# Attention and a nonlocal block in FP32: quarters of q, v and k added by accumulating transfers, another order of steps in a pair, and other readers of the plain product

## The chip, the cores and the metric

The kernel runs on one core of a Trainium2 chip. Its engines work side by side, each on its own queue of instructions: TensorE (PE; its weight loads are shown as PEld), VectorE (DVE), ScalarE (ACT), GpSimd (POOL), and SyncE (SP), which here only issues transfers. Transfers run on 16 DMA engines. TensorE writes to PSUM; VectorE and ScalarE read it from there. The metric is the device time of one execution in microseconds, lower is better. Before the change the median of three runs is 2135.65 us (2135.11 to 2136.66).

## The reference

The input x has 8 images of 512 channels and 32 x 32 positions, all in FP32. Two layers follow each other:

```python
# layer 0: attention with 8 heads of d = 64 over n = 1024 positions
q, k, v = (conv1x1(x, W, b).reshape(B, h, d, n) for W, b in ((Wq, bq), (Wk, bk), (Wv, bv)))
attn = softmax(einsum('bhdn,bhdm->bhnm', q, k) * d ** -0.5, axis=-1)
x = x + conv1x1(einsum('bhnm,bhdm->bhdn', attn, v), Wp, bp)
# layer 1: nonlocal block, then normalization over the batch
g, theta, phi = (conv1x1(x, w, b) for each of the three)      # 256 channels
f = einsum('bcn,bdn->bcd', theta, phi) / n
z = conv1x1(einsum('bcd,bdn->bcn', f, g), W_w, W_b) + x
out = (z - mean(z)) * rsqrt(var(z) + eps) * gamma + beta      # over batch and positions
```

## The kernel before

The images are worked through one after the other. In the loop over `b` (L1008) each image goes through attention; then q, v and k of the *next* image are computed (L1053, L1058, L1069); then the projection of this image's attention output, theta and phi, and the nonlocal block. So there are seven seams, one between each two images, in which q, v and k of the next image are made, and they are the place of this change.

All matrix products by weights use Strassen's scheme in Winograd's form: a product of 2 x 2 blocks by seven block products. For q, v and k of the seams (`six`, L352) it is used twice, one inside the other. The operands' quarters are called 11, 12, 21, 22, and their sums t1 to t4. Of the seven outer products one, 11 by 11, is the *plain product* (`plain`, L373): it goes straight to PSUM in two halves. The other six go in three pairs (`SIX`, L349), the two outer products of a pair side by side; each of them is again seven inner products. A *step* is one of these seven for both members of the pair, and `ORDER` (L350) says in which order the steps come.

An outer product has three accumulators in PSUM, called chains here (the fourth entry of a row of `SEVEN`, L271). Inner products of one chain are added up in place, and after each one VectorE or ScalarE reads the chain as it stands and adds it to (or puts it in) the quarters that need it at that moment. So the next product of a chain can only be written when the last state of it has been read. PSUM is used in four slots of two banks of 512 numbers each. A pair takes all four: chain 0 of member m is in the first bank of slot m, chain 1 in the first bank of slot 2 + m, chain 2 in the second bank of slot 2 + m (L409). The plain product uses two slots just before, and they become slots 2 and 3 of the first pair. In q, a fill between the second and the third pair sums up the softmax denominators in one more slot (L653) and takes their reciprocals (L655); that slot becomes slot 3 of the third pair.

The outer products' results go to the quarters of the result (11, 12, 21, 22) or to two temporary quarters, T6 and T7, which come from a pool of three buffers (`w3`, tag "acc"). The same pool holds the running sums of the exponentials in attention. Once the pairs are done, whole quarters are added to each other (`add`, L370), by GpSimd's elementwise addition of 128 x 1024 numbers: before the third pair 12 += 22 and 12 += T6 (L398, L399); at the end T7 += T6 (only in q), 22 += T7 and 21 += T7 (L431 to L434). In v and k T6 enters T7 when VectorE writes T7 (`third`, L516 and L546).

The plain product's two halves are read twice each (`begin`), for T6 and for 11: three of these reads by ScalarE, the fourth (second half, 11) by VectorE (L388 to L390; L508 in q and k, L545 in v). `fills` puts other work between the steps, in the order of the engine's queue: in q the sums t4 of the next image's x (L252) and the inner sums of t3 and t4 (L264), all on VectorE; in "middle" the denominators and the loads of their reciprocals r, repeated over partitions (L698, SyncE's queue); in v the products of the attention output o with r (L684, GpSimd); in k the sums of o for the projection (L252 and L264, GpSimd).

Instructions that go through `pe`, `dve` or `sp` keep their order in the program on their engine; GpSimd's adds go through `dve` as well, and so have a fixed place in GpSimd's queue. Accumulating transfers are used already for another thing: `together` (L614) puts the four partition groups of a sum of exponentials on each other, one by SyncE and three by GpSimd with `accum_op` (L617).

Of the kernel before, what the change touches and what calls it, by code (L numbers as in the profile page):

```python
# [10 lines left out]
AF = mybir.ActivationFunctionType  # L11
ALU = mybir.AluOpType
# [18 lines left out]
def unshifted(ctx: ExitStack, tc: tile.TileContext, a: dict, out: bass.AP):  # L31
    nc = tc.nc
# [32 lines left out]
    dve = sp = pe  # L65
# [281 lines left out]
                between[n]()  # L347

    SIX = (((1, "21", "11"), (6, "22", "12")), ((3, "t1", "22"), (4, "t2", "T6")), ((5, "t3", "T7"), (2, "t4", "21")))  # L349
    ORDER = (0, 1, 2, 5, 4, 3, 6)  # L350

    def six(name, w, data, positions_out, at, begin, third, fills, by_scalar=False):  # L352

        fills = dict(fills)
        shape = [P, 4, 256] if positions_out else [P, 2, 512]
        temps = {}

        def to(q):
            if q[0] != "T":
                return at(q)  # L360
            if q not in temps:
                temps[q] = w3.tile(shape, F32, tag="acc", name=f"{q}_{name}")
            return temps[q]

        def piece(q, i, j):
            if positions_out:
                return to(q)[:, j * 2:j * 2 + 2, i * P:(i + 1) * P]
            return to(q)[:, i, j * 256:(j + 1) * 256]

        def add(q, of, engine=None):  # L370
            dve((engine or nc.gpsimd).tensor_tensor(to(q), to(q), to(of), ALU.add))

        def plain():  # L373
            d = data["11"]
            for half in range(2):
                ps = next_bank(f"{name}_0_{half}")[:, 0, :]
                if positions_out:
                    ps = ps.rearrange("p (i f) -> p i f", f=256)
                for i in range(2 if positions_out else 1):
                    for k in range(2):  # L380
                        if positions_out:
                            at = (half * 2 + i) * P
                            pe(nc.tensor.matmul(ps[:, i, :], d[:, k, at:at + P], w[:, 0, k, :],  # L383
                                                start=(k == 0 and i == 0), stop=(k == 1), skip_group_check=True))
                        else:
                            pe(nc.tensor.matmul(ps, w[:, 0, k, half * P:(half + 1) * P], d[:, k, :],  # L386
                                                start=(k == 0), stop=(k == 1), skip_group_check=True))
                for q in ("T6", "11"):  # L388
                    at_ = to(q)[:, half * 2:half * 2 + 2, :] if positions_out else to(q)[:, half, :]
                    begin(at_, ps, half, half and q == "11")  # L390
            load_w("first")

        plain()
        for one in fills.pop("plain", ()):
            one()
        for n, pair in enumerate(SIX):
            if n == 2:
                add("12", "22")  # L398
                add("12", "T6")  # L399
                for one in fills.pop("middle", ()):  # L400
                    one()
            slots = [next_bank(f"{name}_in_{n}_{i}") for i in range(4)]
            free[:] = [free[2], free[3], free[0], free[1]]
            begun = set()
            for step, which in enumerate(ORDER):
                _, wi, di, chain, reads = SEVEN[which]
                for m, (outer, of, q) in enumerate(pair):
                    a, d = w.inner(outer)[wi], data[f"inner {of}"][di]
                    ps = slots[m if not chain else 2 + m][:, chain // 2, :256]  # L409
                    start = (m, chain) not in begun  # L410
                    begun.add((m, chain))
                    if positions_out:
                        ps = ps.rearrange("p (i f) -> p i f", f=P)
                        for i in range(2):
                            pe(nc.tensor.matmul(ps[:, i, :], d[:, i * P:(i + 1) * P], a, start=start and not i, stop=True,  # L415
                                                skip_group_check=True))
                    else:
                        pe(nc.tensor.matmul(ps, a, d, start=start, stop=True, skip_group_check=True))  # L418
                    for (i, j), is_first in reads:
                        i, j = int(i) - 1, int(j) - 1  # L420
                        if is_first and q == "T7":
                            third(piece(q, i, j), ps, piece("T6", i, j), i)
                        elif is_first and q not in ("11", "T6"):
                            nc.scalar.copy(piece(q, i, j), ps)  # L424
                        else:
                            dve(nc.vector.tensor_tensor(piece(q, i, j), piece(q, i, j), ps, ALU.add))
                for one in fills.pop((n, step), ()):
                    one()
            load_w()
        assert not fills, fills  # L430
        if by_scalar:  # L431
            add("T7", "T6")
        add("22", "T7")
        add("21", "T7")  # L434

    def rows(q):
        return q[0] if isinstance(q[0], slice) else slice((int(q[0]) - 1) * CC // 2, int(q[0]) * CC // 2)
# [19 lines left out]
    for x_part, w_part in (((0, 1, 0), (w_first[0], 0, 0, 0, 1)), ((1, 2, 0), (w_first[0], 0, 0, 1, 2)),  # L457
# [5 lines left out]
        if w_part:  # L463
            to, m, k, c0, c1 = w_part
            nc.scalar.dma_start(to[:, c0:c1], quarter("WqT", m, k)[:, c0:c1])
    ps = next_bank("warm_ps")[:, 0, :]
# [34 lines left out]
    def heads_of(b, what, w, bias, data, pin=lambda ins: None, steps=None, fills=None, **how):  # L501

        t = mats.tile([P, CC, N], F32, tag=what, name=f"{what}_{b}")

        if fills is not None:
            def begin(to, ps, i, by_vector):
                if by_vector:
                    dve(nc.vector.tensor_scalar(to, ps, bias[:, i:i + 1], 1.0, ALU.add, ALU.mult))  # L508
                else:
                    nc.scalar.activation(to, ps, AF.Identity, bias=bias[:, i:i + 1])  # L510

            def third(to, ps, of, i):
                if what == "q":
                    nc.scalar.activation(to, ps, AF.Identity, bias=steps[:, i:i + 1])
                else:
                    dve(nc.vector.scalar_tensor_tensor(to, ps, steps[:, i:i + 1], of, ALU.add, ALU.add))  # L516

            six(f"p{what}_{b}", w, data, False, lambda q: t[:, rows(q), cols(q)], begin, third, fills,
                what == "q")
            return t  # L520

        def first(q, ps):
            for m in range(2):
                c = rows(q).start + m
                if how.get("early") and q == "21":
                    nc.vector.tensor_scalar(t[:, c, cols(q)], ps[:, m, :], bias[:, c:c + 1], 1.0, ALU.add, ALU.mult)
                else:
                    nc.scalar.activation(t[:, c, cols(q)], ps[:, m, :], AF.Identity, bias=bias[:, c:c + 1])

        seven(f"p{what}_{b}", w, data, False, first, add_to(t, pin), **how)  # L530

        return t

    def values(b, w, data, fills=None):
        v = mats.tile([P, NB, C], F32, tag="v", name=f"v_{b}")

        def at(q):
            return v[:, (int(q[1]) - 1) * NB // 2:int(q[1]) * NB // 2, (int(q[0]) - 1) * C // 2:int(q[0]) * C // 2]

        def as_v(ps):  # L540
            return ps.rearrange("p h (i f) -> p (h i) f", f=C // 2)

        if fills is not None:
            six(f"pv_{b}", w, data, True, at,
                lambda to, ps, _, by_vector: dve(nc.vector.tensor_copy(to, ps)) if by_vector else nc.scalar.copy(to, ps),  # L545
                lambda to, ps, of, _: dve(nc.vector.tensor_tensor(to, of, ps, ALU.add)), fills)  # L546
            return v
        seven(f"pv_{b}", w, data, True, lambda q, ps: nc.scalar.copy(at(q), as_v(ps)),
              lambda q, ps: dve(nc.vector.tensor_tensor(at(q), at(q), as_v(ps), ALU.add)))
        return v  # L550
# [436 lines left out]
    data = {"11": b11, "21": b21, "22": b22, "t1": t[0], "t2": t[1], "t3": t[2], "t4": t[3], "name": "x_0"}  # L987
# [20 lines left out]
    for b in range(B):  # L1008
# [41 lines left out]
        if not last:  # L1050
            data = nxt["data"]
            t3, t4 = (inner_one_by_one(data, of) for of in ("t3", "t4"))
            q = heads_of(b + 1, "q", weights("WqT"), bq, data, dve, steps=dq, fills={  # L1053
                "plain": [lambda: more_sums(data, (4,), dve), t3[0]], (0, 0): t3[1:2], (0, 1): t3[2:3],
                (0, 2): t3[3:], (0, 6): t4[:1], (1, 0): t4[1:2], (1, 1): t4[2:3], (1, 2): t4[3:],
                "middle": [lambda: nxt.update(products=normalize(denominators(next_bank(f"den_{b}"))))]})
            products = nxt["products"]
            v = values(b + 1, weights("WvT"), data, fills={(0, 6): products[:2], (1, 6): products[2:]})  # L1058
# [305 lines left out]
```

## Time and profile before

| | |
|---|---|
| median of 3 runs | 2135.65 us |
| the profiled execution | 2135.05 us, span 2133.3 us |
| PE busy | 2093.9 us, 98% of the span |
| DVE, ACT, POOL busy | 1409.1, 781.1, 526.0 us |
| POOL: adds of quarters (L371) | 91 of 2.35 us, in three groups by tile |
| POOL: accumulating transfers issued (L617) | 189, 0.77 us each |
| accumulating transfer of 128 KB | 3.1 us from issue to landing (median) |
| DMA | 243.56 MB, mean 114 GB/s |

Times in a timeline are microseconds from the start of the span: start, duration, engine, line, operation, output <- inputs, count, and in square brackets how long the engine was idle before it and what ended that. In the view of waits a line gives the total, the number of waits and the longest. In the view of windows, each stretch has its length, then busy time and (x) instructions of PE, PEld, DVE, ACT and POOL, the granted clock, the DMA engines' busy share and GB/s. A matmul's end is modelled, so gaps on PE are best read from starts. FP32 matmuls show as two records each: "x4" is one step of a pair in q or k.

### The profile page before, as it was taken

Reading aid. Unit: us, or ns where it says so; the run is one execution under the profiler, and the core shown is the slowest. Engines: PE = TensorE matmul, PEld = TensorE weight load, DVE = VectorE, ACT = ScalarE, POOL = GpSimd, SP = SyncE. Lnnn points to the kernel's source line nnn. Section 1 sums busy time; section 2 is a strip of 40 time slices with the busy share of each in tenths; the row PEclk is TensorE's granted clock in tenths of the full one; section 3 lists DMA queues with packets and bytes.
Section 4 is the critical chain, followed back from the end, with each engine's and each line's share of the span. In section 5 each row is a group of like instructions: output and inputs, shape, how many; then the busy total and the mean of one; then the engine's idle time right before and its main releaser. Section 6 shows DMA issues by size and latency. Waiting matters only on the chain.

```text
span 2133.3 us, 33255 instructions
## 1 busy us (share of the span) xinstructions
PE 2093.9 (98%) x13486; PEld 1173.4 (55%) x13486; DVE 1409.1 (66%) x2072; ACT 781.1 (37%) x1024; POOL 526.0 (25%) x392
## 2 busy tenths in 40 slices
PE   9999999999999999999999999999999999999995
PEld 4535863358733677336773377633775348743462
DVE  6587567765578655786557766577664775556736
ACT  1464204642046410563105631066312652056116
POOL 0012900128001370014601155011550118111000
PEclk9999999999999999999999999999999999999998
DMA  6253533244232432325324253142543235212768
GB/s 227 84 144 77 172 146 111 38 89 142 99 114 41 105 121 99 117 40 139 101 83 121 41 146 122 50 124 42 152 151 139 41 51 165 92 27 40 235 219 318
DMA packets 71728, 243.56 MB, mean 114 GB/s; under 512 B 12688, under 2 KB 21136, under 8 KB 69520
## 3 DMA queue, kind: packets, MB, share of 16 engines
q1 hardware_dynamic: 60640, 215.01, 30.3%
q0 software_dynamic: 9072, 24.78, 9.5%
q8 instruction: 108, 1.77, 0.3%
q10 hardware_dynamic: 1856, 1.56, 0.3%
q14 instruction: 52, 0.43, 0.1%
HBM read 160.45 MB, written 47.32 MB: 97 GB/s over the span
## 4 chain that ended last, share of the span: by engine, by line
PE 94%; DVE 2%; ACT 2%; DMA 1%; issue 0%; SPq 0%; DVEq 0%; ACTq 0%
PE ps L578 21%; PE po L604 21%; PE ptp L340 9%; PE pp L340 7%; PE pv_in L415 6%; PE pk_in L418 6%; PE pq_in L418 5%; PE pg L340 4%; PE pz L340 3%; PE pf L799 2%; PE pp_in_s L297 2%; PE pq L386 1%; PE pq L340 1%; PE pv L383 1%; PE pv L340 1%; PE pk L386 1%
## 5 line engine op out<-in xcount | busy, mean ns | idle before, releaser
L581 ACT ACTIVATE e<-ps 128x1024 f32<-128x1024 f32 x512 | 523.0, 1025 | 422.8 <-PE ps L578 412.1
L587 DVE TENSOR_TENSOR acc<-acc,e 128x1024 f32<-128x1024 f32 x384 | 469.9, 1224 | 103.6 <-ACT e L581 93.7
L578 PE MATMUL ps<-q,k 64*64 64x512 f32 x4096 | 529.3, 589 | 0.0
L604 PE MATMUL po<-e,v 64*64 64x512 f32 x4096 | 528.7, 589 | 0.0
L617 POOL DMA_DIRECT2D fold<-acc x189 | 144.8, 766 | 1359.1 <-DMA fold<-acc 650.4
L604 PEld LDWEIGHTS po<-e,v 64*64 64x64 f32 x4096 | 156.6, 133 | 282.9 <-issue 275.5
L578 PEld LDWEIGHTS ps<-q,k 64*64 64x64 f32 x4096 | 155.5, 133 | 283.4 <-issue 277.3
L842 ACT ACTIVATE g<-pg,gb 128x512 f32<-128x512 f32 x31 | 21.3, 688 | 442.0 <-PE pg L340 441.9
L585 DVE TENSOR_TENSOR acc<-e,e 128x1024 f32<-128x1024 f32 x64 | 78.3, 1224 | 120.8 <-ACT e L581 118.6
L340 PE MATMUL ptp<-w_tp,t_x 128*128 128x256 f32 x512 | 114.4, 379 | 0.0
L340 PEld LDWEIGHTS ptp<-w_tp,t_x 128*128 128x128 f32 x512 | 97.3, 190 | 13.2
L340 PE MATMUL pp<-t_o,w_WpT 128*128 128x512 f32 x208 | 100.8, 592 | 0.0
L340 PE MATMUL ptp<-w_tp,x 128*128 128x256 f32 x384 | 86.8, 379 | 0.0
L340 PEld LDWEIGHTS ptp<-w_tp,x 128*128 128x128 f32 x384 | 73.0, 190 | 13.3 <-issue 3.8
L340 PE MATMUL pp<-o,w_WpT 128*128 128x512 f32 x144 | 67.8, 593 | 1.9 <-DVE o L684 1.9
L424 ACT COPY v<-pv_in 128x256 f32<-128x256 f32 x84 | 31.3, 372 | 100.8 <-PE pv_in L415 33.1
L424 ACT COPY k<-pk_in 128x256 f32<-128x256 f32 x84 | 31.3, 373 | 97.2 <-PE pk_in L418 96.7
L684 POOL TENSOR_TENSOR o<-o,r 128x1024 f32<-128x1024 f32 x28 | 65.3, 2368 | 0.0
L770 DVE TENSOR_TENSOR tp<-tp,ptp 128x1024 f32<-128x1024 f32 x24 | 29.3, 1221 | 51.2 <-PE ptp L340 51.2
L737 DVE SCALAR_TENSOR_TENSOR x<-pp,bp,x 128x512 f32<-128x512 f32 x52 | 37.6, 746 | 35.0 <-PE pp L340 35.0
L418 PE MATMUL pq_in<-i_t_x,w_WqT 128*128 128x256 f32 x224 | 57.1, 382 | 2.9 <-DVE fold L655 2.9
L424 ACT COPY q<-pq_in 128x256 f32<-128x256 f32 x84 | 31.3, 373 | 76.3 <-PE pq_in L418 75.8
(233 smaller groups left out, 2942.1 us busy)
## 6 DMA issues: line engine op xcount, KB each, us to landing
fold<-acc POOLq DMA_DIRECT2D x189, 128.0 KB, 3.1
w_WqT<-kept_WqT SPq DMA_DIRECT2D x21, 896.0 KB, 4.6
w_WvT<-kept_WvT SPq DMA_DIRECT2D x21, 896.0 KB, 4.9
w_WkT<-kept_WkT SPq DMA_DIRECT2D x21, 896.0 KB, 5.3
r<-den_d SPq DMA_DIRECT2D x32, 512.0 KB, 6.9
x<-in_x_dram SPq DMA_DIRECT2D x30, 512.0 KB, 5.8
spill<-x SPq DMA_DIRECT2D x24, 512.0 KB, 4.0
z<-spill SPq DMA_DIRECT2D x24, 512.0 KB, 10.1
```

The costliest lines, as they stand in the source:

```text
L297: pe(nc.tensor.matmul(ps, a[wi], d[di], start=s not in begun, stop=True, skip_group_check=True))
L340: pe(nc.tensor.matmul(to_ps, lhsT(k), rhs(k), start=(s, at) not in begun, stop=(k == nk - 1), skip_group_check=True))
L415: pe(nc.tensor.matmul(ps[:, i, :], d[:, i * P:(i + 1) * P], a, start=start and not i, stop=True, skip_group_check=True))
L418: pe(nc.tensor.matmul(ps, a, d, start=start, stop=True, skip_group_check=True))
L424: nc.scalar.copy(piece(q, i, j), ps)
L578: pe(nc.tensor.matmul(ps[c * P // 2:(c + 1) * P // 2, j, :], k[r, p, keys], q[r, p, h * 512:(h + 1) * 512], start=True, stop=True, skip_gr ...
L581: nc.scalar.activation(e, ps, AF.Exp, scale=SCALE)
L585: nc.vector.tensor_tensor(accs[u], es[u, 0], e, ALU.add)
L587: ins = nc.vector.tensor_tensor(accs[u], accs[u], e, ALU.add)
L604: pe(nc.tensor.matmul(ps[j * D:(j + 1) * D, r, :], v[keys, m, (2 * p + j) * D:(2 * p + j + 1) * D], e[keys, j, :], start=(m == 0), stop=(m ...
L617: nc.gpsimd.dma_start(to, part_of, accum_op=ALU.add)
L684: dve((engine or nc.vector).tensor_tensor(at, at, of, ALU.mult))
```

## The change

Five things are changed:

1. `add` is an accumulating transfer, issued by GpSimd's queue, from one quarter to the other (512 KB), in place of GpSimd's addition.
2. 12 += T6 goes from its place before the third pair to the end, behind 21 += T7.
3. `ORDER` is 0, 5, 1, 2, 4, 3, 6 in place of 0, 1, 2, 5, 4, 3, 6, and chain 2 of member m is in the second bank of slot m in place of slot 2 + m.
4. All four reads of the plain product are ScalarE's.
5. In q all four inner sums of t3 come right behind t4, ahead of the first pair's reads on VectorE; the four of t4 come behind steps 2, 3 and 6 of the first pair and step 0 of the second.

```diff
-    ORDER = (0, 1, 2, 5, 4, 3, 6)
+    ORDER = (0, 5, 1, 2, 4, 3, 6)
...
-        def add(q, of, engine=None):
-            dve((engine or nc.gpsimd).tensor_tensor(to(q), to(q), to(of), ALU.add))
+        def add(q, of):
+            dve(nc.gpsimd.dma_start(to(q), to(of), accum_op=ALU.add))
...
-                    begin(at_, ps, half, half and q == "11")
+                    begin(at_, ps, half)
...
                 add("12", "22")
-                add("12", "T6")
...
-                    ps = slots[m if not chain else 2 + m][:, chain // 2, :256]
+                    ps = slots[2 + m if chain == 1 else m][:, chain // 2, :256]
...
         add("22", "T7")
         add("21", "T7")
+        add("12", "T6")
...
-            def begin(to, ps, i, by_vector):
-                if by_vector:
-                    dve(nc.vector.tensor_scalar(to, ps, bias[:, i:i + 1], 1.0, ALU.add, ALU.mult))
-                else:
-                    nc.scalar.activation(to, ps, AF.Identity, bias=bias[:, i:i + 1])
+            def begin(to, ps, i):
+                nc.scalar.activation(to, ps, AF.Identity, bias=bias[:, i:i + 1])
...
-                lambda to, ps, _, by_vector: dve(nc.vector.tensor_copy(to, ps)) if by_vector else nc.scalar.copy(to, ps),
+                lambda to, ps, _: nc.scalar.copy(to, ps),
...
-                "plain": [lambda: more_sums(data, (4,), dve), t3[0]], (0, 0): t3[1:2], (0, 1): t3[2:3],
-                (0, 2): t3[3:], (0, 6): t4[:1], (1, 0): t4[1:2], (1, 1): t4[2:3], (1, 2): t4[3:],
+                "plain": [lambda: more_sums(data, (4,), dve), *t3],
+                (0, 2): t4[:1], (0, 3): t4[1:2], (0, 6): t4[2:3], (1, 0): t4[3:],
```

## The prediction, before the result was known

> **What bounds the kernel now.** The page comes first: PE is busy for 98% of the span, at full clock in every slice. Only what makes TensorE wait, or adds work to it, can move the time.
>
> ```profile
> span 2133.3 us, 33255 instructions
> PE 2093.9 (98%) x13486; PEld 1173.4 (55%) x13486; DVE 1409.1 (66%) x2072; ACT 781.1 (37%) x1024; POOL 526.0 (25%) x392
> PEclk9999999999999999999999999999999999999998
> ```
>
> The sum is made on this one execution (2135.05 us, of which 1.75 lies around the span); the runs' median is 2135.65, so what is worked out below is added to that.
>
> Second, who TensorE waited for. The change touches the q, v and k products, and they hold nearly all of it, seven times each (once between two images):
>
> ```profile
> PE pq_in L418 <- DVE q L426: 7.7, 7, 1.1
> PE pq_in L418 <- DVE fold L655: 2.9, 7, 0.6
> PE pk_in L418 <- DVE k L508: 1.9, 7, 0.3
> PE pq_in L418 <- DVE q L508: 1.9, 7, 0.3
> ```
>
> These counts are too small, since a matmul's modelled end covers part of a gap. So, third, the timeline of the seam 448 to 545 us (the other six look the same), where starts are compared with the pace of undisturbed steps: 0.86 us per step in q and k, 0.89 in v (a step is one of the seven of a pair: two products).
>
> ```profile
> 454.36 1.03 PE L418 MATMUL pq_in<-x,w_WqT 128*128 128x256 f32 x4
> 455.22 0.59 PE L418 MATMUL pq_in<-i_x,w_WqT 128*128 128x256 f32 x2
> 456.08 0.70 PE L418 MATMUL pq_in<-i_x,w_WqT 128*128 128x256 f32 x2 [0.27 <-DVE q L508]
> 457.88 1.13 PE L418 MATMUL pq_in<-i_x,w_WqT 128*128 128x256 f32 x4 [1.10 <-DVE q L426]
> 458.85 1.03 PE L418 MATMUL pq_in<-x,w_WqT 128*128 128x256 f32 x4
> ...
> 455.28 0.75 DVE L508 TENSOR_SCALAR q<-pq,bq 128x512 f32<-128x512 f32 x1 [3.02 <-ACT T_pq L510]
> 455.95 1.22 DVE L252 TENSOR_TENSOR t_x<-x,t_x 128x1024 f32<-128x1024 f32 x1
> 457.42 0.41 DVE L426 TENSOR_TENSOR q<-q,pq_in 128x256 f32<-128x256 f32 x1
> ```
>
> To be seen: VectorE stands for 3.02 us before its read of the plain product, then does that, t4 and an inner sum, and only then the read (457.42) that step 2 of TensorE waits for.
>
> Fourth, POOL's timeline and the windows' DMA share:
>
> ```profile
> 476.57 2.35 POOL L371 TENSOR_TENSOR T_pq<-T_pq,T_pq 128x1024 f32<-128x1024 f32 x1 [3.22 <-ACT T_pq L514]
> 479.00 4.68 POOL L371 TENSOR_TENSOR q<-q,T_pq 128x1024 f32<-128x1024 f32 x2
> 483.63 9.32 POOL L684 TENSOR_TENSOR o<-o,r 128x1024 f32<-128x1024 f32 x4
> ...
> 480.00:486.00 6.00, 5.94 (x53) 5.75 (x53) 4.20 (x10) 1.60 (x4) 6.00 (x4) 1.00 0.98 230
> ```
>
> To be seen: q's last three adds end at 483.6, ten microseconds before anything needs them; and just there (480 to 486) the 16 DMA engines are 98% busy, with r and WkT.
>
> **What is removed.** In q, steps 0 to 2 take 458.85 - 454.36 = 4.49 us where 2.59 would do: 1.90. Behind the denominators two steps take 2.38 (470.41 to 472.79) instead of 1.72: 0.66. In v steps 0 to 2 take 3.01 (479.70 to 482.71) instead of 2.68: 0.33. In k 3.13 (502.22 to 505.35) instead of 2.59: 0.54. Together 3.43 per seam, 24.0 us in all. Do they all go? Step 1 now writes the second bank of a slot that is free, so the slots of the plain product (and the denominators' bank, free at 471.35) are first written in step 2: 456.08 and 456.51 for the two products of q. ScalarE's fourth read starts one pitch (0.59) after 454.56 and ends at 455.85; in k it ends near 503.7 against 503.94. VectorE, with no read to stand for, can do t4 from 452.27 (end of L610) and the four sums of t3 after it (some 0.37 each): done near 455.1, when its first read falls due (454.36 + 0.43 + 0.2). The moved t4 sums (3 x 0.42) lie beside ten reads (4.2) in a pair of 6.0 us: no price, but only 0.5 us of cover.
>
> **What the order adds.** By the list of steps the old order takes the accumulators 0,1,0,2,0,1,0; the new one 0,2,1,0,0,1,0. Steps 3 and 4 write the same accumulator back to back, and step 4 may not write before step 3 is read. No row shows this, but its parts are there: one product lasts 0.43, a reader starts 0.20 behind it (DVE 510.73 after a product that ended at 510.52), reads for 0.42 (VectorE), 0.37 or 0.47 (ScalarE), and TensorE goes on 0.05 later (457.83 to 457.88). 0.43 + 0.20 + 0.42 + 0.05 = 1.10 against a step of 0.86: 0.24, and 0.10 for the weight load that each stall lays bare (458.85 - 457.88 = 0.97). By reader: q 0.34 + 0.30 + 0.39, k 0.34 + 0.30 + 0.40, v (products of 0.447) 0.33 + 0.28 + 0.33. That is 3.01 per seam, 21.1 us in all; 15 if the weight load hides, 27 if VectorE is 0.1 behind each time. The balance so far is -2.9.
>
> **What the transfers add.** 91 adds of 2.35 us leave POOL; each becomes an issue (0.77 by the row of fold) and 512 KB of accumulating traffic, and the end of the last now counts. Issue to first packet is 1.33 us in the packets of fold. Fold's 128 KB then take 1.01 to 1.48, so 512 KB would take 4.0 to 5.9; plain 4096-byte packets take 0.159, eight per engine 1.3. Fold touches 32 partitions; r touches 64 and moves 8192 bytes in 0.616, half the pace of the plain packets over 128. So I take half of fold's slow case, 2.8 us (0.35 per 4096 bytes), if nothing runs beside it.
>
> After q something does. T7 += T6 is issued at 476.57 less the 1.5 us that q is then shorter: 475.05. From 476.4 its eight packets per engine alternate with r's: 8 x (0.35 + 0.616) = 7.7, landed at 484.2. POOL stands at 22 += T7 until then (behind it on its queue: 21 += T7, 12 += T6, now moved here from the middle, and the products o x r, which begin near 487 instead of 483.6). First packet of 22 at 485.5; 22 and 21 need 5.6 us of each engine, and some 6 us of r's rest and WkT lie between: 21 has landed near 497.
>
> Who waits for that? The pool of T6, T7 and the attention's sums has three buffers: q holds two, v's T6 the third, so v's T7 can be written only when 21 += T7 has landed (it reads q's T7). That write (L546, 493.24 before, 491.9 now with all shifts) is VectorE's; TensorE follows it two steps later, so it may start up to 493.0 at no cost. 497 - 493 = 4.0 us per seam, 28 in all. Bounds: nothing (landing by 493), and 8 us if the pool hands out q's T6, which 12 += T6 holds longest.
>
> The rest is covered: 12 += 22 of q lands near 473; v's adds land near 516 and k's T7 is written near 519; the o sums on POOL move from 503.6 to about 508, and the project products need the inner ones of o from about 530, when the first are ready by 521; k's adds have 50 us to the scores; the loads of WkT have 10 us to spare.
>
> The Trainium skill speaks otherwise on the price: "DMA: Bandwidth & Descriptors", section on the anatomy of one DMA, fits a GpSimd-issued transfer by 2.0 us + bytes/436e3, an estimate of 3.2 us for 512 KB; by that chain 21 += T7 would be in by about 485 and the sum would be -2.9. The same page, section "Queues, rings and completion order", has each DMA engine take turns between queues packet by packet; that is the alternation used above, and the trace shows its like: the accumulation issued at 138.66, beside loads, took 8.2 us to land where 2.3 to 2.8 is usual.
>
> Sum: -24.0 + 21.1 + 28 = +25: 2160 us.
>
> **Rivals.** (1) The transfers stay hidden: 21 += T7 lands before 493.0. That needs some 4 us less from 475.05 on, as with 0.2 us per packet or if r's packets, slow by themselves, let others through. For it: an engine held by a half-rate stream may have room; against: the share of 0.98. Then -2.9, between -9 and +3 by the bounds of the order's stall: 2133. (2) The pool hands out the later buffer, or k's T7 waits as well: 8 us per seam, 2189. For it: 12 += T6 is last on the queue; against: a free-list would give the first one freed. (3) POOL becomes the bound: if an issue grows with its runs (256 of 2 KB against fold's 32), 0.77 becomes 6.1, the three after T7 += T6 end near 502, the products near 512, v's four near 536, the o sums and inner ones near 551 against 530: some 18 us per seam, 2260. Against it: nothing but that fold's issue varies little (0.756 to 0.908); no row has more runs.
>
> **How the numbers follow.** Mine 0.50; (1) 0.33; (2) 0.12; (3) 0.05. A measurement here tells 0.2% (4.3 us) from no change. Rival 1 lies around that line: 0.17 faster, 0.13 the same, 0.03 slower; all others are slower, 0.70. The range takes in (1) but for its last bit and (2): 2128 to 2190; what I call likeliest alone spans 2142 to 2180.
>
> **What would show it.** TensorE's waits for DVE q L508, k L508, q L426 of step 2 and fold L655 gone; in their place waits of 0.2 to 0.4 us in step 4 of each pair, 63 in all; VectorE waiting for a DMA of q's adds before the first T_pv of the third pair of v, and TensorE in the same place; POOL idle until T_pq has landed, 8 us or more after its issue. I am wrong if step 4 starts on time (another accumulator, or a reader that is faster), or if the landing of 21 += T7 is before 493 on this clock.

## The result, and the profile after

The changed kernel takes 2245.9 us (median of four runs, 2245.29 to 2251.22) against 2135.8 before: a ratio of 1.0521, 95% interval 1.0503 to 1.0539. That is 110 us slower, where 24 us were forecast, and 56 us above the upper end of the range. The profiled execution took 2245.60 us, with a span of 2243.8; the sums below are made on its span against the 2133.3 us of before.

The page of the kernel after (span; busy times; the granted clock of TensorE in 40 slices; GpSimd's transfer queue with its packets, MB and share; the chain that ended last, by engine):

```profile
span 2243.8 us, 33407 instructions
...
PE 2139.8 (95%) x13486; PEld 1184.1 (53%) x13486; DVE 1401.2 (62%) x2051; ACT 790.0 (35%) x1045; POOL 424.2 (19%) x392
...
PEclk9999899999999999999999999999999999999998
...
q0 software_dynamic: 40096, 72.50, 21.3%
...
PE 87%; DMA 7%; ACT 2%; DVE 2%; issue 1%; POOL 0%; DVEq 0%; SPq 0%; POOLq 0%; ACTq 0%
```

TensorE has the same 13486 matmuls, so all of the 110 us is standing still, or the same work done more slowly. Transfers now hold 7% of the chain that ended last. GpSimd's queue moves 40096 packets instead of 9072. TensorE's busy time has risen by 45.9 us with no work added. Of this 29.3 us are there too in the kernel with GpSimd's adds (2123.2 us busy, clock 0.996 as before), where short waits hide under modelled ends; the rest comes with a lower clock. The clock by slices hides it: a slice is 56 us long, and only the mean over the whole run tells (0.978 of full speed, 0.996 before).

Where the time went, by phases of TensorE (from the start of a phase's first matmul to the start of the next phase's, summed over the kernel):

| us | before | after |
|---|---|---|
| q | 203.6 | 202.7 |
| v | 182.0 | 276.5 |
| k | 178.7 | 192.2 |
| projection | 189.5 | 192.6 |
| attention | 880.5 | 880.5 |
| theta, phi and the nonlocal block | 493.1 | 493.5 |

So q gained next to nothing although 1.5 us per seam were to go there (2.56 less 1.03 for the order), k lost 1.9 us per seam, and v lost 13.5 us per seam.

The waits of the kernel after (engine, line, tile, what it waited for: total, number, longest):

```profile
PE pv_in L414 <- DVE T_pv L543: 67.6, 7, 10.6
DVE T_pv L543 <- DMA q<-T_pq: 67.3, 7, 10.5
```

The seven waits are where the prediction put them: VectorE's first write of v's T7 (L543 now, L546 before) waits for an accumulating transfer of q, and TensorE stands behind it. Only they last 9.7 us each, not 4.0.

The chain that ended last, through q and v of the second seam (start, duration, what):

```profile
470.88 0.45 PE pq_in L417 x2
471.42 0.43 DVE q L425
471.89 2.61 PE pq_in L417 x10
474.53 0.43 DVE q L425
475.00 3.72 PE pq_in L417 x16
...
493.02 11.88 DMA T_pq<-T_pq
...
505.45 0.72 POOL q L371
506.17 13.15 DMA q<-T_pq
519.40 0.43 DVE T_pv L543
519.88 4.65 PE pv_in L414 x20
```

Two things are to be seen. At the start of a pair (470 to 475 us) the chain goes *twice* through a read by VectorE, not once. And from 493.02 to 519.40 the path is GpSimd's transfers alone: T7 += T6, then the issues behind it, then 21 += T7.

### The profile page after: what moved, and what is told of

It is laid out like the page before. It is cut to its first block, busy times and chain, and to the rows that moved or that the text cites. A ratio compares the mean times of both kernels' runs of the same rounds, so it can differ in the third digit from the quotient of the medians.

```text
span 2243.8 us, 33407 instructions
## 1 busy us (share of the span) xinstructions
PE 2139.8 (95%) x13486; PEld 1184.1 (53%) x13486; DVE 1401.2 (62%) x2051; ACT 790.0 (35%) x1045; POOL 424.2 (19%) x392
## 3 DMA queue, kind: packets, MB, share of 16 engines
q0 software_dynamic: 40096, 72.50, 21.3%
## 4 chain that ended last, share of the span: by engine, by line
PE 87%; DMA 7%; ACT 2%; DVE 2%; issue 1%; POOL 0%; DVEq 0%; SPq 0%; POOLq 0%; ACTq 0%
PE ps L575 20%; PE po L601 20%; PE ptp L340 9%; PE pp L340 7%; PE pk_in L417 6%; PE pq_in L417 6%; DMA q<-T_pq 4%; PE pg L340 4%; PE pv_in L414 3%; PE pz L340 3%; DMA T_pq<-T_pq 2%; PE pf L796 2%; PE pp_in_s L297 2%; PE pq L386 1%; PE pq L340 1%
## 5 line engine op out<-in xcount | busy, mean ns | idle before, releaser
L414 PE MATMUL pv_in<-w_WvT,t_x 128*128 128x128 f32 x336 | 52.6, 306 | 67.7 <-DVE T_pv L543 67.6
L414 PEld LDWEIGHTS pv_in<-w_WvT,t_x 128*128 128x128 f32 x336 | 46.9, 214 | 70.4 <-DVE T_pv L543 69.0
L425 DVE TENSOR_TENSOR v<-v,pv_in 128x256 f32<-128x256 f32 x112 | 46.4, 421 | 56.6 <-PE pv_in L414 54.1
L425 DVE TENSOR_TENSOR k<-k,pk_in 128x256 f32<-128x256 f32 x112 | 46.8, 421 | 49.5 <-PE pk_in L417 47.5
L681 POOL TENSOR_TENSOR o<-o,r 128x1024 f32<-128x1024 f32 x28 | 75.0, 3808 | 0.0
## 6 DMA issues: line engine op xcount, KB each, us to landing
w_WkT<-kept_WkT SPq DMA_DIRECT2D x21, 896.0 KB, 10.2
```

Of the source, the lines that this page charges most:

```text
L681: dve((engine or nc.vector).tensor_tensor(at, at, of, ALU.mult))
```

## The experiments

Three theories are used. *Reads*: what the change takes away is worth the 24.0 us of the forecast. *Waits by bank* (the forecast's) against *waits by slot*: a product waits for the last read of its own accumulator, or for the last read of anything in its slot of two banks. *Buffer*: v waits for the buffer that q's T7 holds, against a DMA system that slows everything.

### GpSimd adds again, all else as changed

```diff
-            dve(nc.gpsimd.dma_start(to(q), to(of), accum_op=ALU.add))
+            dve((engine or nc.gpsimd).tensor_tensor(to(q), to(q), to(of), ALU.add))
```

> The changed kernel, but the quarters are added by GpSimd's additions again (all else as changed, 12 += T6 at the end too). Theory (slots and buffer): two losses lie over each other, the waits that the new order brings and the wait of v's T7 for a buffer. Here only the first is left: 126 waits of 0.41 us less the 24 us that the other parts save, so 2163 us (2157 to 2169), and no wait of VectorE for a transfer in v. Rival (all of the loss belongs to the transfers, the order costs what the prediction said): about 2133 us.

Measured: 2162.99 us, ratio 1.0127 (1.0110 to 1.0144). In the phases: q 202.3, v 194.7, k 193.2, projection 189.5. So the transfers account for 84.0 of the 110.5 us (span 2159.8), 81.8 of it in v and 3.1 in the projection, and the rest of the change loses 26.5 us by itself, where the forecast had a gain of 2.9. TensorE's view of waits hardly shows this loss:

```profile
PE pk_in L417 <- DVE T_pk L513: 1.5, 7, 0.2
PE pq_in L417 <- DVE q L425: 1.1, 7, 0.2
PE pk_in L417 <- DVE k L425: 1.1, 7, 0.2
```

Each line gives 0.2 us at most. What the waits cost is to be read from starts, because a matmul's modelled end covers most of a gap that is shorter than the matmul. From start to start, against the undisturbed pace, step 4 comes 0.33 to 0.41 us late in each of the 63 pairs (22.4 us in all), and step 1, for which no wait was forecast, 0.33 to 0.59 (27.8 us). All other steps keep the pace, but for 0.2 us per seam beside the denominators that the kernel before has too.

### The transfers alone, in the kernel before

```diff
-            dve((engine or nc.gpsimd).tensor_tensor(to(q), to(q), to(of), ALU.add))
+            dve(nc.gpsimd.dma_start(to(q), to(of), accum_op=ALU.add))
...
-                add("12", "T6")
...
         add("21", "T7")
+        add("12", "T6")
```

> The kernel before with the transfers alone (adds as accumulating transfers, 12 += T6 at the end). Theory: v's T7 waits for q's buffer in each seam, some 9 us, and 2.3 us more go to a lower clock behind the wait: 2136 + 7 x 11.3 = 2215 us (2200 to 2230); k as long as before (22.1 us). Rival (the order's waits carry the loss): below 2160 us.

Measured: 2225.6 us, ratio 1.0415 (1.0397 to 1.0432): 89.1 us more than before. v takes 270.1 us, q and k 204.3 and 178.7 as before.

```profile
DVE T_pv L546 <- DMA q<-T_pq: 77.6, 7, 11.8
```

The same wait at the same place, with the old order and the old readers. So the wait for the buffer needs nothing of the rest of the change.

### The reads and the sums of x alone

```diff
-                    begin(at_, ps, half, half and q == "11")
+                    begin(at_, ps, half)
...
-                "plain": [lambda: more_sums(data, (4,), dve), t3[0]], (0, 0): t3[1:2], (0, 1): t3[2:3],
-                (0, 2): t3[3:], (0, 6): t4[:1], (1, 0): t4[1:2], (1, 1): t4[2:3], (1, 2): t4[3:],
+                "plain": [lambda: more_sums(data, (4,), dve), *t3],
+                (0, 2): t4[:1], (0, 3): t4[1:2], (0, 6): t4[2:3], (1, 0): t4[3:],
```

> The kernel before with only the plain product read by ScalarE and the sums of t3 and t4 ahead; old order, old places, GpSimd's additions. Theory: nearly all waits of the first pair go in q and half of those in k; the second product of step 1 still waits some 0.2 to 0.3 us for ScalarE's last read, and the wait behind the denominators stays: 7 x 2.1 = 14 us less, 2121 us (2118 to 2126). Rival (what the prediction counted as removed needs the new order): within 3 us of 2136.

Measured: 2121.66 us, ratio 0.9938 (0.9921 to 0.9954), 14.8 us less than the kernel before beside it (2136.46). It is the part of the change that gains. With the old order TensorE's wait behind the denominators stays, and the others in q are gone from its list of waits, which now begins with

```profile
PE pq_in L418 <- DVE fold L652: 2.9, 7, 0.6
```

By the starts, step 1 of the first pair is still 0.33 us late in q and k and 0.09 in v, as the expectation had it: 5.3 us over the seams, which the list does not show.

### The place of chain 2 alone

Against the kernel of the last experiment, with the *old* order of steps, in which no accumulator follows itself:

```diff
-                    ps = slots[m if not chain else 2 + m][:, chain // 2, :256]
+                    ps = slots[2 + m if chain == 1 else m][:, chain // 2, :256]
```

> The kernel with ScalarE's reads and the sums ahead (old order, GpSimd's additions: 2121.7 us), and chain 2 put in the second bank of slot m in place of slot 2 + m, nothing else. In this order no chain follows itself. Theory (a write waits for the last read of the slot, both banks together): the slots of the steps are now A, B, A, A, A, B, A, two waits per pair, 126 of some 0.41 us: 2173 us (2160 to 2185). Rival (a write waits for its own bank alone, as the prediction took it): 2122 us (2118 to 2126).

Measured: 2166.83 us, ratio 1.0147 (1.0130 to 1.0164), 45.2 us more than with the old place. Only the place differs, and every accumulator still has another one between two of its products. In this order chain 2 stands between two products of chain 0 (the accumulators come as 0, 1, 0, 2, 0, 1, 0), so two steps of each pair now write a slot whose other bank was written just before: 2 x 3 pairs x 3 products x 7 seams = 126, or 0.36 us each. TensorE in this kernel, the first pair of q (start, duration, line, operation, tiles, count of records):

```profile
459.74 2.22 PE L418 MATMUL pq_in<-i_x,w_WqT 128*128 128x256 f32 x8
462.04 1.13 PE L418 MATMUL pq_in<-x,w_WqT 128*128 128x256 f32 x4
463.25 1.13 PE L418 MATMUL pq_in<-i_x,w_WqT 128*128 128x256 f32 x4
464.21 1.03 PE L418 MATMUL pq_in<-x,w_WqT 128*128 128x256 f32 x4
```

and in the kernel it was made from:

```profile
453.68 2.22 PE L418 MATMUL pq_in<-i_x,w_WqT 128*128 128x256 f32 x8
455.73 1.03 PE L418 MATMUL pq_in<-x,w_WqT 128*128 128x256 f32 x4
456.59 1.03 PE L418 MATMUL pq_in<-i_x,w_WqT 128*128 128x256 f32 x4
457.46 0.81 PE L418 MATMUL pq_in<-x,w_WqT 128*128 128x256 f32 x3
```

From the first start to the last are four steps: 464.21 - 459.74 = 4.47 us with the new place and 457.46 - 453.68 = 3.78 with the old one, 0.69 for two waits. So the waits are set by slot. They are semaphore waits that the program carries, for the tile; the runs don't show that the banks themselves hinder each other. No run has the new order with the old place.

### Another buffer for v's T7

```diff
-                temps[q] = w3.tile(shape, F32, tag="acc", name=f"{q}_{name}")
+                if positions_out and q == "T7":
+                    temps[q] = block(f"{q}_{name}").rearrange("p a (i f) -> p (a i) f", f=256)
+                else:
+                    temps[q] = w3.tile(shape, F32, tag="acc", name=f"{q}_{name}")
```

The block comes from a ring that other stages share. Its slots are handed out in turn, so this also moves which block others get.

> The changed kernel, but v's T7 has a buffer of its own (a free block of the ring of exponentials), so that it need not wait for q's T7. Theory: VectorE's wait in v is gone, and with it the lower clock: v some 25 us per seam instead of 36, 2246 - 7 x 11 = 2168 us (2160 to 2180), transfers as slow as before. Rival (the transfers are too slow in themselves and the wait only moves to the next user, k's T6 or T7 or the projection): above 2200 us.

Measured: 2175.38 us, ratio 1.0182 (1.0165 to 1.0199), 70.5 us less than the changed kernel. v falls from 276.5 to 194.2 us, which is its time with GpSimd's adds. That is the proof for the buffer: the transfers are the same, and 21 += T7 still lands 27.0 to 29.5 us after the issue of T7 += T6. What remains over the run with GpSimd's adds is 12.4 us, and it lies in k (206.1 against 193.2):

```profile
ACT T_pk L510 <- DMA q<-T_pq: 20.7, 6, 5.3
...
PE pk_in L420 <- DVE k L428: 9.3, 7, 3.2
```

With one buffer less asked of the pool by v, k's T6 gets one that a late transfer of q still reads, and waits in its turn: in this part the rival was right.

### Half of the loads that run beside

Only half of r is loaded, and that half used twice, so the attention output is scaled by the wrong halves; nothing else changes.

```diff
-            for k in range(2):
+            for k in range(1):
...
-            return [lambda k=k, h=h: product(..., r[:, k, h],
+            return [lambda k=k, h=h: product(..., r[:, 0, h],
```

> The changed kernel, but only the first half of r is loaded (two of four transfers of 512 KB) and used for both halves, so the output is that of wrong denominators for half of the positions; the instructions of the engines are the same. Theory (T7 += T6 shares the DMA engines with r, and the next ones with what r has pushed back): T7 += T6 lands 3 to 4 us earlier, 21 += T7 some 5 us, and the wait in v is shorter by that: 7 x 5 = 35 us less, 2211 us (2195 to 2225). Rival (the chain of landings is slow by itself): 2246 us.

Measured: 2203.34 us, ratio 1.0315 (1.0294 to 1.0335), 42.6 us less than the changed kernel. v takes 236.3 us, and the wait falls to less than half:

```profile
DVE T_pv L543 <- DMA q<-T_pq: 30.6, 7, 9.5
```

So the loads of r share the DMA engines with the accumulations, at the expense of these. But the place is another than the theory's: T7 += T6 lands only 1.1 us earlier in the mean (11.8 to 10.7 us after its issue; 3 to 4 were expected), its first packet still comes 2.8 to 5.6 us after the issue, and the rest is gained in 22 += T7 and 21 += T7.

### The first add of the row of three by GpSimd

```diff
         if by_scalar:
-            add("T7", "T6")
+            dve(nc.gpsimd.tensor_tensor(to("T7"), to("T7"), to("T6"), ALU.add))
```

> The changed kernel with T7 += T6 of q alone given back to GpSimd (2.35 us), all other adds by transfers. Theory (the first landing, 11.9 us, stands in front of the others): 22 += T7 and 21 += T7 are issued some 9.5 us earlier, but then share the DMA engines with r, so 21 += T7 lands about 5 us earlier, near 514 on the clock of the changed kernel: 7 x 5 = 35 us less, 2211 us (2190 to 2225). Rival (it is the bytes in total that count, not the chain): within 10 us of 2246.

Measured: 2217.45 us, ratio 1.0384 (1.0367 to 1.0402), 28.4 us less than the changed kernel.

```profile
DVE T_pv L543 <- DMA q<-T_pq: 39.4, 7, 6.4
```

GpSimd's add takes 2.35 us where the transfer took 11.9, yet the wait shortens by 4.0 us per seam only (67.3 to 39.4 over seven). The two transfers that are left meet the loads all the same: the first packet of 22 += T7 now comes 6.9 to 7.2 us after its issue. The chain of transfers counts, and so does what they meet.

### The buffer held longer, with no transfers

In the kernel before, eight more additions by GpSimd of T6 to q's T7 after its last use. Nothing reads what they make.

```diff
         add("21", "T7")
+        if by_scalar:
+            for _ in range(8):
+                add("T7", "T6")
```

> The kernel before, with T7 and T6 of q held longer by GpSimd (eight additions more on T7 after its last use, 18.8 us), no transfers in place of additions. Theory (a buffer that comes late, and a lower clock for some 10 us behind any gap of TensorE of such length): VectorE waits some 9 us before v's first write of T7, TensorE 7 to 8 us, and 2.2 us go to the clock: 7 x 10 = 70 us more, 2206 us (2190 to 2215), with the clock at a half behind each gap. Rival (the lower clock comes with the transfers): full clock throughout, 2190 us or less.

Measured: 2216.29 us (one run; the kernel before beside it 2136.62). v takes 262.6 us, 80.6 more than before, or 11.5 us per seam. By the starts the gap is 9.3 of these, and the other 2.2 are the clock behind it. The windows of the second seam:

```profile
512.00:514.00 2.00, 0.00 (x0) 0.00 (x0) 0.00 (x0) 0.00 (x0) 1.92 (x2) 0.50 0.00 0
514.00:516.00 2.00, 0.79 (x3) 0.79 (x4) 0.75 (x2) 0.00 (x0) 2.00 (x2) 0.50 0.00 0
516.00:518.00 2.00, 2.00 (x12) 2.00 (x11) 0.42 (x1) 0.37 (x1) 2.00 (x2) 0.50 0.00 0
518.00:520.00 2.00, 2.00 (x13) 2.00 (x13) 1.08 (x3) 0.00 (x0) 2.00 (x2) 0.63 0.00 0
520.00:522.00 2.00, 2.00 (x19) 1.99 (x18) 1.83 (x5) 0.00 (x1) 2.00 (x2) 1.00 0.00 0
```

DMA stands still throughout (the last two columns), TensorE is idle until 515.2, and the clock stays at half for some four more microseconds of full work: 12 matmul records in 516 to 518 where 520 to 522, at full clock, has 19. So a long wait alone makes the clock drop; no transfer is needed for it.

### A version that keeps what gains

Against the kernel with the reads and sums alone: ScalarE copies the denominators out of PSUM and VectorE takes the reciprocal of the copy, so that the bank is free sooner.

```diff
-            dve(nc.vector.reciprocal(ri, den))
+            nc.scalar.copy(ri, den)
+            dve(nc.vector.reciprocal(ri, ri))
```

> The kernel with ScalarE's reads and the sums ahead (2121.7 us), and the denominators copied from PSUM by ScalarE before VectorE takes the reciprocals of the copy. Theory (the wait behind the denominators is for their bank, which the reciprocal holds for 1.76 us; the copy holds it for some 0.4): 0.6 us per seam go, 7 x 0.6 = 4 us less, 2117.5 us (2115 to 2120). Rival (the reads behind the reciprocal on VectorE's queue are what TensorE waits for): within 2 us of 2121.7.

Measured: 2117.18 us, ratio 0.9914 (0.9897 to 0.9930). That is 4.5 us less than with the reads and sums alone, 18.7 less than the kernel before beside it (2135.83), and faster than both kernels. No wait of pq_in, pv_in or pk_in is left in TensorE's list, though by the starts the 5.3 us of step 1 in the first pairs are still there. q takes 187.7 us instead of 203.6.

## Why the prediction was wrong, by its own steps

**What is removed: 24.0 us.** This term held. By the starts the kernel before loses 24.0 us at these places, and in the kernel with GpSimd's adds none of the waits for the plain product's slots or the denominators' bank is left: step 2 starts on time. Of the term, the reads and sums gave 14.8, with the denominators' bank it was 18.7, and the other 5.3 are the late step 1 of the first pairs, which goes where that step no longer writes the plain product's slots.

**What the order adds: 21.1 us. It was 50.** This step failed first. The one wait that it counted, of step 4 for the read of step 3, is there at about the price worked out: 0.36 us each against 0.335, 22.4 us in all. What failed is the sentence "Step 1 now writes the second bank of a slot that is free". That bank lies in the slot whose first bank step 0 has just written, and by slot (A for slot m, B for slot 2 + m) the new order goes A, A, B, A, A, B, A. So step 1 waits for the read of step 0, and this second wait, which was put at nothing, cost 27.8 us. In the first pair of q and k it is longest, since ScalarE is then still reading the plain product. TensorE at the start of the pair in the kernel after, and VectorE's read:

```profile
470.71 1.03 PE L417 MATMUL pq_in<-x,w_WqT 128*128 128x256 f32 x4
471.89 1.30 PE L417 MATMUL pq_in<-x,w_WqT 128*128 128x256 f32 x4 [0.15 <-DVE q L425]
473.03 3.10 PE L417 MATMUL pq_in<-i_x,w_WqT 128*128 128x256 f32 x12
475.97 1.03 PE L417 MATMUL pq_in<-x,w_WqT 128*128 128x256 f32 x4
...
471.42 0.42 DVE L425 TENSOR_TENSOR q<-q,pq_in 128x256 f32<-128x256 f32 x1 [0.20 <-PE pq_in L417]
```

From 470.71 to 475.97 lie five steps, 4.32 us at the undisturbed pace of 0.864; they take 5.26. With two waits per pair there are 126 in all, not 63, of 0.40 us in the mean, against 0.36 in the run that moves the chain alone. With GpSimd's adds -24.0 + 50.2 = +26.2 us, where 26.5 were measured.

**What the transfers add: 28 us, 4.0 per seam. It was 84.0.** The buffer was the right one: 21 += T7, which reads q's T7, and not 12 += T6, which landed at 521.88, 2.5 us after VectorE's write had begun. The times from the issue of T7 += T6, forecast and measured in the second seam and over all seven:

| us after the issue of T7 += T6 | forecast | measured | seven seams |
|---|---|---|---|
| its first packet | 1.3 | 5.3 | 2.7 to 5.4 |
| T7 += T6 landed | 9.1 | 11.9 | 10.2 to 13.4 |
| first packet of 22 += T7 | 10.5 | 16.9 | 15.7 to 17.5 |
| 21 += T7 landed | 22 | 26.3 | 26.3 to 27.8 |
| latest start of VectorE's write at no cost | 18.0 | 17.4 | |

(The 17.4: TensorE's gap of 8.98 us before 519.88 begins at 510.90, and it starts 0.48 behind VectorE, with step 1 and not "two steps later".) The path was as forecast, and so was the rate of the accumulation: 0.327 us per packet of 4096 bytes in T7 += T6, against 0.35, and in a quiet stretch the 16 packets of 2048 bytes per engine (12 += 22 of k) take 2.9 us from first to last, against 2.8. The failed sub-step is "issue to first packet is 1.33 us": beside the loads of r and of WkT it was 2.7 to 5.4 us for T7 += T6 and 3.5 to 5.0 for 22 += T7. The trace of before had shown it: the accumulation issued at 138.66 beside loads, which the forecast itself names, had its first packet 5.1 us after the issue. The Trainium skill, on which the forecast leaned here ("DMA: Bandwidth & Descriptors", section "Queues, rings and completion order"), has each DMA engine take turns between the queues for which it has work, packet by packet. From the first packet on the trace is in keeping with that: from 498.3 to 503.4 packets of both queues run beside each other. For the time before it no run shows whether the packets were in a queue yet. The estimate of 3.2 us by the page's fit (section on the anatomy of one DMA) is too low here: even in the quiet stretch the last packet ended 4.7 us after the issue, and the transfer landed after 5.0.

GpSimd's issues and products of the seam, with what it waited for:

```profile
493.02 0.90 POOL L371 DMA_DIRECT2D T_pq<-T_pq  x1 [6.91 <-ACT T_pq L511]
505.45 3.67 POOL L371 DMA_DIRECT2D q<-T_pq  x3 [11.53 <-DVE v L425]
507.66 10.71 POOL L681 TENSOR_TENSOR o<-o,r 128x1024 f32<-128x1024 f32 x4
```

In brackets stands VectorE's read, which ended about then; the chain, which has the landing at 504.91, shows what held GpSimd. And the windows of TensorE's stand (the last two columns are the DMA engines' share and GB/s):

```profile
502.00:508.00 6.00, 5.97 (x50) 5.59 (x49) 3.33 (x9) 1.49 (x4) 2.55 (x4) 1.00 1.02 308
508.00:514.00 6.00, 2.89 (x26) 2.70 (x25) 1.93 (x5) 0.74 (x2) 6.00 (x4) 1.00 1.07 287
514.00:520.00 6.00, 0.12 (x1) 0.12 (x1) 0.42 (x1) 0.00 (x0) 5.63 (x3) 0.51 1.09 271
520.00:526.00 6.00, 5.94 (x32) 5.75 (x33) 1.91 (x5) 0.75 (x2) 0.00 (x0) 0.63 0.62 91
```

The DMA engines are full from 502 to 520; the accumulations and the loads share them until 517, and then the accumulations have them alone.

**A term that was left out: the clock, some 15 us.** Of the 81.8 us that v takes more than with GpSimd's adds (11.7 per seam), the gaps are 9.5 by the starts. The other 2.2 per seam are the granted clock (2.2 too in the run without transfers), which falls to half during the gap and stays there after TensorE resumes (0.51 and 0.63 in the windows above: 32 matmuls in 6 us, with TensorE busy throughout, where 502 to 508 has 50). A gap of the forecast's 4.0 us would not have been spared: in the runs with half of r and with GpSimd's first add there are seven gaps of 2.5 to 4.8 us, and behind six of them the steps took 1.6 to 2.5 us longer, behind one nothing. The sum of the 84.0: 28 forecast, 38.5 for a gap of 9.5 in place of 4.0, 15 for the clock, 3.1 in the projections, and -0.6 in q and k.

**What the projections lose, and what stays open.** The 3.1 us are all in the last projection (29.28 instead of 26.16), and it is longer, by 2.0 to 3.1 us, in three other runs with transfers too. The traces settle it: in exactly these four the clock was half for 3.4 us behind TensorE's pause there (2.2 to 3.3 us), which is 1.7 us of work, and the rest is the pause itself (3.28 us against 1.86, in the changed kernel). In all others the pause is 1.8 to 2.6 us and the clock stays full. The pause grew because r landed in 8.2 instead of 6.5 us; why it did is open. Why the first packets stand for 3 to 5 us, in the DMA engines or ahead of them, was not settled either; halving r shows only that the load beside them counts.

**The rivals.** Hidden transfers (1) fell: a landing before 493.0 on that clock was missed by 8 us. The later buffer (2) was the wrong mechanism, though nearer in size. In (3) an issue was to grow from 0.77 to 6.1 us: it took 0.90 us with 128 runs and up to 2.77 with 512, and issues followed each other by 0.73 to 0.75 us, so GpSimd did not become the bound. The sign was right, and so was the buffer; both sizes were too small by more than a factor of two, the order's by a wait that was not counted, the transfers' by the first packets and the clock.

## What to carry to other kernels

When accumulators change places, list for each step which *tile* it writes and which tile the step before wrote: the waits follow the tile, and two accumulators in one tile follow each other like one. When an elementwise add becomes a transfer, its operands' buffers are held from issue to landing under the load of that moment, so ask who gets the buffer next, and take the first packet's delay from a row beside the same loads, not from a quiet one. Add to a gap of TensorE what the clock takes behind it: here some 2 us, whether the gap was 3 us long or 10. A gain of 24 us on the path was lost to waits of 0.4 us that the list of waits shows as 0.2 or not at all: count steps by their starts.

## What the runs showed of the hardware that was not expected

- After gaps of TensorE of 9.0 to 10.9 us in v (22 in four runs, by the modelled ends) the granted clock was half for 10.2 us, in four of them for 13.7, part of it after work had resumed. After seven gaps of 5.0 to 6.5 us it was half for 6.8, once for 10.2; after six of 2.6 to 3.9, for 3.4 or 6.8, and once not at all. Behind all but that one the steps took 1.4 to 3.0 us longer, and behind the short gaps hardly less than behind the long ones. The lengths are multiples of 3.41 us. The Trainium skill, "TensorE: Matmul & The Clock Gate", says the like (Part 1: a free-running window of 3413 ns), and these runs agree; its advice of no gaps of more than about 3 us (section "Why this matters for your kernels") is no sharp line here, as gaps of 2.2 to 2.7 us were followed by half clock in some places and not in others.
- Accumulating packets take longer than plain ones of their size in other transfers (medians): 0.327 us for 4096 bytes in T7 += T6 of q (0.159 plain), 0.178 for 2048 (0.084), 0.102 for 1024 (0.046).
- From a transfer's last data packet to its landing 0.3 us pass in a quiet stretch (12 += 22 of k), and 1.4 to 1.8 for T7 += T6 of q, beside the loads. Of the 16 packets of 4 bytes that close 21 += T7, fifteen start by 517.71 and the last at 518.96; the transfer landed at 519.32.
- GpSimd's products o x r took 3.81 us each in the records where 2.37 was usual, and four of them 10.7 us instead of 9.3, while its transfers were being issued and moved beside them. The records overlap, so the first number is not a pace.
